# Group averages through small resident matrices, and a last convolution stage in four parts, in a fused channel-attention and selective-scan kernel

## The chip, the cores and the metric

The kernel runs on one core of one Trainium2 chip, in fp32 throughout. The metric is the device time of one execution in microseconds (us), as the median of several runs. TensorE (PE) does products, VectorE (DVE), ScalarE (ACT) and GpSimd (POOL) do elementwise work, and SyncE (SP) issues nearly all DMAs. Each engine takes its own instructions in order and waits on semaphores for the others.

## The reference

The input x is 8 images of 384 channels and 64 x 64 pixels. Two residual layers follow one another, each behind a group normalisation with 32 groups of 12 channels:

```
# layer 0
g = group_norm(x)                      # 32 groups of 12 channels
q, k, v = (dwconv3x3(conv1x1(g, w), dw) for each of the three)
attn = softmax(l2norm(q) @ l2norm(k).T * temperature)   # 8 heads, 48 x 48 channels each
x = x + conv1x1(attn @ v, wproj)
# layer 1
g = group_norm(x)
y = selective_scan of g in four directions (row, column, and both reversed), 16 states
x = x + gelu(layer_norm_over_channels(y merged))
```

A group's mean is the mean of its 12 channels' means; its variance is the mean over the 12 channels of (channel variance + squared distance of the channel mean from the group mean).

## The kernel before, in words

The eight images (batches) run one after another. The 384 channels are three blocks of 128 partitions (NJ = 3, indices j and m), and an image is three resident tiles x[j] of 128 x 4096 elements.

**Attention** (`channel_attention`) runs for one batch at a time. `norm_factors` turns per-channel statistics into mean and rstd per channel. It loads a 384 x 384 averaging matrix avg (576 KB, L113), aggregates the statistics on DVE (L116), multiplies avg with the channel means on PE (L124: seven products, those of each block and its neighbours, since groups of 12 straddle blocks), forms the distance of each channel's mean (L128 to L131), multiplies avg with that (L136, seven products again), and takes the root on ACT (L141). An fp32 product appears in the trace as two PE instructions. Then the 1x1 weights are scaled by rstd (L195), and the three convolutions k, q, v follow. A piece of a convolution (`conv`) is a run of products (L223), their evacuation by ACT (L228), the centre tap on ACT (L232) and eight taps on DVE (L244), each a pass over the whole piece. k and q use pieces of 64 or 32 rows. v is done in three parts, of rows 0 to 32, 32 to 48 and 48 to 64, each for the three blocks; an edge row is carried from one part to the next, and every part but the last computes one row more than it writes.

Woven into the v stage are two other things. `project_out` multiplies the attention matrix, already folded with wproj into mT, with 512 columns of v (L353: three products, one for each block of v), adds the result to x on DVE (L358), takes its statistics (L359) and stores it (L360). A part's projections are put on a list and taken off it, six at a time, during the next part; what is left on the list after the last part is done at the end. And for batches 1 to 7 `finish_part` (L872 to L894) completes 1/16 of the previous batch's layer 1: two loads, scaling on ACT, transposes on PE (L888), gelu on ACT (L889), an add on DVE (L893) and a store. Two of these are emitted behind each of the first eight pieces of v, in two shared buffers. `token_norm` (L862 to L869) takes the statistics for them earlier, from loads fy of the previous batch's result.

**The scan** (`selective_scan`) then calls `norm_factors` with the new statistics, scales x in place (L421, L426), and works through 32 steps of 8 periods each. Its order is written out by hand and pinned. In its last periods it loads the next batch's x and takes its statistics. Its last act is to store y (L658).

Outside the scan a planner decides the order on each engine: it takes instructions by program order and by when it reckons that their inputs are ready, and the order it finds is then fixed. Buffers are shared by tag; an instruction that writes a shared buffer waits for the last reader of the earlier content, and the tiles of a stage wait for the memory of the stage before. The tag "wt" has two buffers, used in turn by avg (in the attention's call of `norm_factors`), wk, wq, wv and wproj. The convolutions and the projections share three PSUM banks (tag "pc").

Of the kernel before, what the change touches and what calls it, by code (L numbers as in the profile page):

```python
# [9 lines left out]
F32 = mybir.dt.float32  # L10
# [5 lines left out]
P = 128  # L16
C = 384
NJ = C // P
H = W = 64
L = H * W  # L20
CH = 512
# [1 line left out]
NT = L // P  # L23
HEADS = 8
HC = C // HEADS
GROUP = C // 32
K = 4
R = 12
N = 16
# [11 lines left out]
GN_EPS = 1e-5  # L41
# [13 lines left out]
BW = max(hi - lo for lo, hi in BANDS)  # L55
# [7 lines left out]
def _constants():  # L63

    c = np.arange(C)
    same = (c[:, None] // GROUP == c[None, :] // GROUP).astype(np.float32)
    avg = (same / np.float32(GROUP)).reshape(NJ, P, C).transpose(1, 0, 2)
    mask = np.zeros((P, NJ, BW), np.float32)
    for i, (lo, hi) in enumerate(BANDS):
        rows = (i * P + np.arange(P)) // HC  # L70
        cols = (lo + np.arange(BW)) // HC
        mask[:, i] = np.where(rows[:, None] == cols[None, :], 0.0, MASKED)
    return np.ascontiguousarray(avg), mask


@with_exitstack
def tile_channel_attention_then_selective_scan(ctx: ExitStack, tc: tile.TileContext, a: dict):
# [10 lines left out]
    pair = const.tile([P, HP], F32, name="pair")  # L88
    twos = ident.rearrange("p (l v) -> p l v", v=2)
    nc.vector.tensor_add(pair, twos[:, :, 0], twos[:, :, 1])  # L90
    ones = const.tile([P, P], F32, name="ones")
    nc.gpsimd.memset(ones, 1.0)
    eps = const.tile([P, 1], F32, name="eps")
# [13 lines left out]
    for j in range(NJ):  # L107
        nc.vector.tensor_scalar_mul(skip[:, j, :], ident, d_sum[:, j : j + 1])

    def norm_factors(pool, psum, stats, tag, bank, home={}):  # L110

        avg = pool.tile([P, NJ, C], F32, name=f"avg{tag}", **home)
        nc.sync.dma_start(avg, a["avg"])  # L113
        mv = pool.tile([P, NJ, 2], F32, name=f"mv{tag}")
        for j in range(NJ):
            nc.vector.bn_aggr(mv[:, j, :], stats[:, j].rearrange("p c s -> p (c s)"))  # L116
        mean = pool.tile([P, NJ], F32, name=f"mean{tag}")
        rstd = pool.tile([P, NJ], F32, name=f"rstd{tag}")
        var = pool.tile([P, NJ], F32, name=f"var{tag}")
        pm = psum.tile([P, CH], F32, tag=bank, name=f"pm{tag}")  # L120
        for j in range(NJ):
            src = [i for i in range(NJ) if abs(i - j) <= 1]
            for i in src:
                nc.tensor.matmul(  # L124
                    pm[:, j : j + 1], lhsT=avg[:, i, j * P : (j + 1) * P], rhs=mv[:, i, 0:1],
                    start=i == src[0], stop=i == src[-1],
                )
        nc.vector.tensor_copy(mean, pm[:, 0:NJ])  # L128
        nc.vector.tensor_sub(var, mv[:, :, 0], mean)
        nc.vector.tensor_mul(var, var, var)  # L130
        nc.vector.tensor_add(var, var, mv[:, :, 1])  # L131
        pv = psum.tile([P, CH], F32, tag=bank, name=f"pv{tag}")
        for j in range(NJ):
            src = [i for i in range(NJ) if abs(i - j) <= 1]
            for i in src:
                nc.tensor.matmul(  # L136
                    pv[:, j : j + 1], lhsT=avg[:, i, j * P : (j + 1) * P], rhs=var[:, i : i + 1],
                    start=i == src[0], stop=i == src[-1],
                )
        nc.vector.tensor_scalar_add(rstd, pv[:, 0:NJ], GN_EPS)  # L140
        nc.scalar.activation(rstd, rstd, AF.Sqrt)  # L141
        nc.vector.reciprocal(rstd, rstd)
        return mean, rstd
# [19 lines left out]
    def channel_attention(b, x, stats, before):  # L163
# [5 lines left out]
        with ExitStack() as st:  # L169
# [4 lines left out]
            ps_a = st.enter_context(tc.tile_pool(name=f"pa{b}", bufs=2, space=PSUM))  # L174
            ps_m = st.enter_context(tc.tile_pool(name=f"pm{b}", bufs=1, space=PSUM))

            mean, rstd = norm_factors(wp, ps_m, stats, f"0_{b}", "misc", dict(tag="wt", bufs=2))

            dws = {}
            for n in ("k", "q", "v"):  # L180
# [94 lines left out]
            for m in range(NJ):  # L275
                acc = work.tile([P, L], F32, tag="acc", name=f"ak{b}{m}")
                parts = (0, H // 2, H) if m == 0 else (0, H)
                for y0, y1 in zip(parts, parts[1:]):
                    conv("k", wk, bk, m, y0, y1, acc[:, y0 * W : y1 * W])
                for t4 in range(NT // 4):  # L280
                    to_tokens(acc, t4, kT[:, 4 * t4 : 4 * t4 + 4, bass.ts(m, P)], f"k{b}{m}")
                r = inverse_norm(acc, f"k{b}{m}")
                diag = work.tile([P, P], F32, tag="diag", name=f"diag{b}{m}")
                nc.vector.tensor_scalar_mul(diag, ident, r)
                pr = ps_a.tile([P, CH], F32, tag="pa", name=f"pr{b}{m}")
                nc.tensor.matmul(pr[:, :P], lhsT=ones, rhs=diag, start=True, stop=True)
                nc.scalar.copy(rks[:, bass.ts(m, P)], pr[:, :P])
# [4 lines left out]
            for m in range(NJ):  # L292
                lo, hi = BANDS[m]
                wd = hi - lo
                acc = work.tile([P, L], F32, tag="acc", name=f"aq{b}{m}")
                parts = (0, H // 2, H) if m == NJ - 1 else (0, H)
                for y0, y1 in zip(parts, parts[1:]):
                    conv("q", wq, bq, m, y0, y1, acc[:, y0 * W : y1 * W])
                pa = ps_a.tile([P, CH], F32, tag="pa", name=f"pa{b}{m}")
                for t4 in range(NT // 4):  # L300
                    qT = work.tile([P, 4, P], F32, tag="qT", name=f"qT{b}{m}_{t4}")
                    to_tokens(acc, t4, qT, f"q{b}{m}")
                    for i in range(4):
                        t = 4 * t4 + i
                        nc.tensor.matmul(
                            pa[:, :wd], lhsT=qT[:, i, :], rhs=kT[:, t, lo:hi],
                            start=t == 0, stop=t == NT - 1,
                        )
                r = inverse_norm(acc, f"q{b}{m}")
                nc.vector.tensor_mul(r, r, small["temp"][:, m : m + 1])  # L310
                lg = work.tile([P, BW], F32, tag="lg", name=f"lg{b}{m}")
                nc.vector.tensor_mul(lg[:, :wd], pa[:, :wd], rks[:, lo:hi])
                nc.vector.scalar_tensor_tensor(
                    lg[:, :wd], lg[:, :wd], r, mask[:, m, :wd], ALU.mult, ALU.add
                )
                mx = work.tile([P, 1], F32, tag="mx", name=f"mx{b}{m}")
                nc.vector.reduce_max(mx, lg[:, :wd], axis=AX.X)
                nc.vector.tensor_scalar_mul(mx, mx, -1.0)
                sm = work.tile([P, 1], F32, tag="sm", name=f"sm{b}{m}")
                nc.scalar.activation(lg[:, :wd], lg[:, :wd], AF.Exp, bias=mx, accum_out=sm)  # L320
                nc.vector.reciprocal(sm, sm)
                nc.vector.tensor_scalar_mul(attn[:, m, lo:hi], lg[:, :wd], sm)
# [24 lines left out]
            x1_d = dram.tile([NJ, P, L], F32, tag="x1d", bufs=2, name=f"x1d{b}")  # L347
            stats1 = big.tile([P, NJ, NCH, nc.vector.BN_STATS_DIM], F32, tag="st1", name=f"st1{b}")

            def project_out(m, c):  # L350
                pc = ps_c.tile([P, CH], F32, tag="pc", name=f"pp{b}{m}_{c}")
                for j in range(NJ):
                    nc.tensor.matmul(  # L353
                        pc, lhsT=mT[:, j, bass.ts(m, P)], rhs=v[:, j, bass.ts(c, CH)],
                        start=j == 0, stop=j == NJ - 1,
                    )
                s = x[m][:, bass.ts(c, CH)]
                nc.vector.tensor_add(s, s, pc)  # L358
                nc.vector.bn_stats(stats1[:, m, c, :], s)  # L359
                nc.sync.dma_start(x1_d[m, :, bass.ts(c, CH)], s)  # L360


            parts = (0, H // 2, 3 * H // 4, H)
            todo, left, edges = [], list(range(L // FT)) if emit else [], {}
            for y0, y1 in zip(parts, parts[1:]):
                for m in range(NJ):
                    pre = conv("v", wv, bv, m, y0, y1, v[:, m, y0 * W : y1 * W], edges.get(m))
                    if y1 < H:
                        edges[m] = work.tile([P, W], F32, tag="edge", bufs=4, name=f"edge{b}{m}_{y1}")
                        o = (y1 - 1 - max(0, y0 - 1)) * W  # L370
                        nc.scalar.copy(edges[m], pre[:, o : o + W])
                    if m > 0:
                        for _ in range(min(len(todo), 6)):
                            project_out(*todo.pop(0))
                    for _ in range(min(len(left), 2)):
                        emit(left.pop(0))
                todo += [(m, c) for c in range(y0 * W // CH, y1 * W // CH) for m in range(NJ)]
            for t in todo:
                project_out(*t)
        return x, x1_d, stats1  # L380

    def selective_scan(b, x1, stats1):
# [535 lines left out]
def _layout(i):  # L918
    def blocks(t, lead):
# [2 lines left out]
        return np.ascontiguousarray(t.reshape(NJ, P, *t.shape[1:]).swapaxes(0, 1))  # L922

    i = {k: np.asarray(v) for k, v in i.items()}
    avg, mask = _constants()
    B = i["x"].shape[0]
    return {
        "x": np.ascontiguousarray(i["x"]).reshape(B, NJ, P, L),
# [13 lines left out]
        "ln_w": blocks(i["L1_conv_ln_weight"], 0),  # L942
        "ln_b": blocks(i["L1_conv_ln_bias"], 0),
        "ident": np.eye(P, dtype=np.float32),
        "avg": avg,
        "mask": mask,
    }

# [16 lines left out]
```

## Time and profile before

| | |
|---|---|
| median of 3 runs (lowest to highest) | 20747.19 us (20741.09 to 20748.04) |
| the profiled execution's own time | 20748.06 us |
| its span, first to last instruction | 20746.3 us |
| PE busy | 19205.9 us (93%) |
| DVE busy | 19321.9 us (93%) |
| ACT busy | 17951.9 us (87%) |
| POOL busy | 15441.2 us (74%) |
| mean granted clock of PE | 0.969 |

The shares are averages over two kinds of stage: POOL has 3.4 us of work in 466 us of a batch's attention and is busy nearly all through the scan. So a stage's limit has to be read from that stage. In the lines below, a time is in us from the start of the span; a line of the timeline has its start, its duration, engine, line, operation, output and input tiles, the count of merged instructions, and in brackets how long the engine stood idle ahead of it and what ended that. Digits in a tile's name are the batch (pc7v: the v convolution of batch 7). PEld is PE's weight load. The ends of products are modelled, so sums of durations on PE overlap a little. A wait on several things is put down to the one that came last by the profile, which need not be the one that mattered.

### The profile page before, as it was taken

The page shows a single profiled execution, that of the slowest core. Times are in us where ns is not written, and L with a number is a line of the kernel's source. Part 1 is how long each engine was busy: PE and PEld are TensorE (multiplying, and loading weights), DVE is VectorE, ACT ScalarE, POOL GpSimd, SP SyncE. Part 2 cuts the span into 40 slices and gives each one's busy share as a digit, 9 for nine tenths or more (in the row PEclk, how much of TensorE's full clock was granted, in tenths as well). Part 3 has the DMA queues.
Part 4 walks back from the last instruction along what each step waited for, and adds up shares of the span by engine and source line. Part 5 has one row for each costly group of instructions (what it writes and reads, how often), then busy time and mean ns, then how long its engine had stood idle before and what let it go on. Part 6 is the DMA issues. An engine that isn't in the chain of part 4 may idle for free. (4 is left out here: it accounts for less than half of the span.)

```text
span 20746.3 us, 319602 instructions
## 1 busy us (share of the span) xinstructions
PE 19205.9 (93%) x118256; PEld 10578.6 (51%) x118256; DVE 19321.9 (93%) x17310; ACT 17951.9 (87%) x32267; POOL 15441.2 (74%) x6918
## 2 busy tenths in 40 slices
PE   7999979999899998999989999899998999989998
PEld 4555545555455554555545555455554555545554
DVE  8999989999899998999989999899998999989998
ACT  3999949999599995999859998599985999859998
POOL 0899808998189981899819997199972999729997
PEclk8999989999899998999989999899998999989999
DMA  1232322323223232232322323223232232322223
GB/s 40 76 92 92 101 77 77 92 93 101 75 80 92 92 104 70 80 92 93 105 68 80 92 92 105 70 80 92 92 103 71 81 93 92 98 74 82 92 92 117
DMA packets 953164, 1807.96 MB, mean 87 GB/s; under 512 B 125905, under 2 KB 646353, under 8 KB 945457
## 3 DMA queue, kind: packets, MB, share of 16 engines
q1 hardware_dynamic: 950736, 1787.40, 27.2%
q8 instruction: 933, 15.29, 0.3%
q14 instruction: 631, 5.16, 0.1%
q10 hardware_dynamic: 864, 0.12, 0.0%
HBM read 1468.39 MB, written 318.77 MB: 86 GB/s over the span
## 5 line engine op out<-in xcount | busy, mean ns | idle before, releaser
L557 POOL TENSOR_TENSOR db<-w,B 128x1536 f32<-128x1536 f32 x4088 | 14143.8, 3467 | 566.6 <-DVE h L569 238.8
L569 DVE TENSOR_TENSOR_SCAN h<-da,ca,db 128x512 f32<-128x512 f32 x10752 | 13058.6, 1267 | 500.2 <-issue 204.3
L603 ACT ACTIVATE hc<-pt,ct 128x384 f32<-128x384 f32 x15128 | 8437.0, 579 | 346.5 <-PE pt L591 287.5
L548 ACT ACTIVATE da<-dt,neg_a 128x512 f32<-128x512 f32 x12288 | 8504.5, 695 | 166.3 <-DVE h L569 134.2
L591 PE MATMUL pt<-ident,h 128*128 128x128 f32 x49152 | 7976.9, 287 | 457.5 <-ACT hc L603 305.0
L591 PEld LDWEIGHTS pt<-ident,h 128*128 128x128 f32 x49152 | 5145.5, 140 | 5115.7 <-ACT hc L603 2549.8
L626 PE MATMUL py<-hc,pair 128*64 128x384 f32 x24576 | 5327.1, 512 | 9.1 <-DVE ys L677 9.1
L406 POOL MEMSET wdt<- 128x1536 f32 x8 | 11.0, 1378 | 3621.5 <-DMA x1d<-x 3621.5
L569 DVE TENSOR_TENSOR_SCAN h<-da,db 128x512 f32<-128x512 f32 x1536 | 1811.5, 1231 | 145.2 <-ACT da L548 75.6
L632 PE MATMUL py<-hc,pair 128*64 128x128 f32 x24576 | 1871.6, 281 | 0.0
L626 PEld LDWEIGHTS py<-hc,pair 128*64 128x64 f32 x24576 | 1216.6, 135 | 1014.6 <-issue 945.3
L455 PE MATMUL px<-x,wx 128*44 128x128 f32 x6144 | 1501.7, 338 | 35.4 <-ACT x L421 29.1
L632 PEld LDWEIGHTS py<-hc,pair 128*64 128x64 f32 x24576 | 1377.2, 136 | 267.2 <-issue 240.2
L532 POOL TENSOR_TENSOR w<-x,dt 128x512 f32<-128x512 f32 x744 | 1057.9, 1422 | 0.0
L455 PEld LDWEIGHTS px<-x,wx 128*44 128x44 f32 x6144 | 635.0, 121 | 817.1 <-issue 771.9
L583 POOL COPY ca<-h 128x6 f32<-128x6 f32 x1792 | 344.2, 192 | 828.4 <-DVE h L569 817.2
L514 PE MATMUL pd<-xd,wdt 128*128 128x512 f32 x1536 | 781.5, 618 | 87.6 <-ACT hc L603 81.8
L605 DVE TENSOR_SCALAR hc<-pt,ct 128x384 f32<-128x384 f32 x1256 | 741.1, 607 | 106.2 <-PE pt L591 61.1
L353 PE MATMUL pp<-v,mT 128*128 128x512 f32 x1152 | 553.9, 634 | 123.5 <-DVE v L244 57.3
L524 ACT ACTIVATE dt<-pd,dt_bias 128x512 f32<-128x512 f32 x768 | 475.4, 686 | 21.3 <-PE pd L514 17.7
L514 PEld LDWEIGHTS pd<-xd,wdt 128*128 128x128 f32 x1536 | 275.3, 192 | 401.3 <-ACT hc L603 199.7
L353 PEld LDWEIGHTS pp<-v,mT 128*128 128x128 f32 x1152 | 228.3, 205 | 403.0 <-issue 312.1
(315 smaller groups left out, 11713.7 us busy)
## 6 DMA issues: line engine op xcount, KB each, us to landing
B<-bcd SPq DMA_DIRECT2D x2048, 512.0 KB
yd<-ys SPq DMA_DIRECT2D x128, 576.0 KB
ys<-yd SPq DMA_DIRECT2D x256, 288.0 KB
yd<-ys SPq DMA_DIRECT2D x256, 288.0 KB
x<-in_x SPq DMA_DIRECT2D x48, 1024.0 KB
x1d<-x SPq DMA_DIRECT2D x192, 256.0 KB
fy<-yd SPq DMA_DIRECT2D x128, 384.0 KB
fin<-yd SPq DMA_DIRECT2D x112, 384.0 KB
```

The source lines that it names most:

```text
L353: nc.tensor.matmul(pc, lhsT=mT[:, j, bass.ts(m, P)], rhs=v[:, j, bass.ts(c, CH)], start=j == 0, stop=j == NJ - 1,)
L455: pin(nc.tensor.matmul(split(pxs[s][:XR, :])[:, part, :], lhsT=wx[:, j, k, :], rhs=view(x1[j], k, c)[:, part, :], start=i == 0, stop=i == ...
L514: pin(nc.tensor.matmul(pds[j], lhsT=wdt[:, k, bass.ts(j, P)], rhs=xds[s], start=True, stop=True))
L532: pin(eng.tensor_mul(split(ws[s][:, j, :]), view(x1[j], k, c), split(dts[s][:, j, :])))
L548: pin(nc.scalar.activation(t, dts[s][:, j, :], AF.Exp, scale=neg_a[:, j, k, n : n + 1]))
L557: pin(eng.tensor_mul(t, ws[g // NP], bts[g][:, v : v + 1, :].broadcast_to([P, NJ, CH])))
L569: pin(nc.vector.tensor_tensor_scan(h, da, db, 0.0 if start else carries[s - 1][:, j, n : n + 1], ALU.mult, ALU.add,))
L591: pin(nc.tensor.transpose(t[:, bass.ts(j, P)], h2s[g][:, j, bass.ts(q, HP), :].rearrange("p l v -> p (l v)"), ident))
L603: pin(eng.activation(out, src, AF.Copy, scale=scale))
L605: pin(eng.tensor_scalar_mul(out, src, scale))
L626: pin(nc.tensor.matmul(py[f * HP : (f + 1) * HP, lb, :C], lhsT=pair, rhs=hc[:, f, :], **flags))
L632: pin(nc.tensor.matmul(py[f * HP : (f + 1) * HP, j, C:], lhsT=pair, rhs=hc[:, f, bass.ts(j, P)], **flags,))
```

## The change

It has four pieces.

- **Group averages.** avg is gone. Two small matrices are loaded once at the start, on SP ahead of x: to_groups (384 channels to 32 groups, with the factor 1/12) and from_groups (32 groups back to 384 channels). An average is now three accumulating products into 32 partitions, a copy on DVE to SBUF, and three products back. Both are done for the mean and for the variance, so each call of `norm_factors` has twelve products where it had fourteen, two more copies, and no load.
- **v in four parts:** rows 0 to 32, 32 to 48, 48 to 56 and 56 to 64. The list then holds three projections at the end, where it held six.
- **The last projections** are one call of `project_out` for all three places: it issues the products of blocks 0 and 1 of v for each of the three, then those of block 2, then the adds.
- **Room:** the work tiles diag and lg have one buffer where they had two.

```diff
-    def norm_factors(pool, psum, stats, tag, bank, home={}):
-        avg = pool.tile([P, NJ, C], F32, name=f"avg{tag}", **home)
-        nc.sync.dma_start(avg, a["avg"])
+    to_groups = const.tile([P, NJ, GROUPS], F32, name="to_groups")
+    nc.sync.dma_start(to_groups, a["to_groups"])
+    from_groups = const.tile([GROUPS, C], F32, name="from_groups")
+    nc.sync.dma_start(from_groups, a["from_groups"])
...
+    def norm_factors(pool, psum, stats, tag, bank):
...
-        pm = psum.tile([P, CH], F32, tag=bank, name=f"pm{tag}")
-        for j in range(NJ):
-            src = [i for i in range(NJ) if abs(i - j) <= 1]
-            for i in src:
+        def average(src, name):
+            pg = psum.tile([P, CH], F32, tag=bank, name=f"{name}g{tag}")
+            for j in range(NJ):
                 nc.tensor.matmul(
-                    pm[:, j : j + 1], lhsT=avg[:, i, j * P : (j + 1) * P], rhs=mv[:, i, 0:1],
-                    start=i == src[0], stop=i == src[-1],
+                    pg[:GROUPS, :1], lhsT=to_groups[:, j, :], rhs=src[j],
+                    start=j == 0, stop=j == NJ - 1,
                 )
-        nc.vector.tensor_copy(mean, pm[:, 0:NJ])
+            g = pool.tile([GROUPS, 1], F32, name=f"{name}s{tag}")
+            nc.vector.tensor_copy(g, pg[:GROUPS, :1])
+            pm = psum.tile([P, CH], F32, tag=bank, name=f"{name}{tag}")
+            for j in range(NJ):
+                nc.tensor.matmul(
+                    pm[:, j : j + 1], lhsT=from_groups[:, bass.ts(j, P)], rhs=g,
+                    start=True, stop=True,
+                )
+            return pm[:, :NJ]
+        nc.vector.tensor_copy(mean, average([mv[:, j, 0:1] for j in range(NJ)], "pm"))
...
-            mean, rstd = norm_factors(wp, ps_m, stats, f"0_{b}", "misc", dict(tag="wt", bufs=2))
+            mean, rstd = norm_factors(wp, ps_m, stats, f"0_{b}", "misc")
...
-                diag = work.tile([P, P], F32, tag="diag", name=f"diag{b}{m}")
+                diag = work.tile([P, P], F32, tag="diag", bufs=1, name=f"diag{b}{m}")
...
-                lg = work.tile([P, BW], F32, tag="lg", name=f"lg{b}{m}")
+                lg = work.tile([P, BW], F32, tag="lg", bufs=1, name=f"lg{b}{m}")
...
-            def project_out(m, c):
-                pc = ps_c.tile([P, CH], F32, tag="pc", name=f"pp{b}{m}_{c}")
-                for j in range(NJ):
-                    nc.tensor.matmul(
...
+            def project_out(*places):
+                pcs = {}
+                for m, c in places:
+                    pcs[m, c] = ps_c.tile([P, CH], F32, tag="pc", name=f"pp{b}{m}_{c}")
+                for js in ((0, 1), (2,)):
+                    for m, c in places:
+                        for j in js:
+                            nc.tensor.matmul(
+                                pcs[m, c], lhsT=mT[:, j, bass.ts(m, P)], rhs=v[:, j, bass.ts(c, CH)],
+                                start=j == 0, stop=j == NJ - 1,
+                            )
+                for m, c in places:
+                    s = x[m][:, bass.ts(c, CH)]
+                    nc.vector.tensor_add(s, s, pcs[m, c])
+                    nc.vector.bn_stats(stats1[:, m, c, :], s)
+                    nc.sync.dma_start(x1_d[m, :, bass.ts(c, CH)], s)
...
-            parts = (0, H // 2, 3 * H // 4, H)
+            parts = (0, H // 2, 3 * H // 4, 7 * H // 8, H)
...
-                            project_out(*todo.pop(0))
+                            project_out(todo.pop(0))
...
-            for t in todo:
-                project_out(*t)
+            assert len(todo) == NJ
+            project_out(*todo)
```

More of the change, by code (lines that the diff above doesn't have):

```diff
@@ L25 @@
 HC = C // HEADS
-GROUP = C // 32
+GROUPS = 32
+GROUP = C // GROUPS
 K = 4
@@ L65, in _constants @@
     c = np.arange(C)
-    same = (c[:, None] // GROUP == c[None, :] // GROUP).astype(np.float32)
-    avg = (same / np.float32(GROUP)).reshape(NJ, P, C).transpose(1, 0, 2)
+    member = (c[:, None] // GROUP == np.arange(GROUPS)[None, :]).astype(np.float32)
+    to_groups = (member / np.float32(GROUP)).reshape(NJ, P, GROUPS).transpose(1, 0, 2)
     mask = np.zeros((P, NJ, BW), np.float32)
@@ L72, in _constants @@
         mask[:, i] = np.where(rows[:, None] == cols[None, :], 0.0, MASKED)
-    return np.ascontiguousarray(avg), mask
+    return np.ascontiguousarray(to_groups), np.ascontiguousarray(member.T), mask
 @with_exitstack
@@ L131, in norm_factors @@
         nc.vector.tensor_add(var, var, mv[:, :, 1])
-        pv = psum.tile([P, CH], F32, tag=bank, name=f"pv{tag}")
-        for j in range(NJ):
[L134 to L140, printed above, removed]
+        nc.vector.tensor_scalar_add(
+            rstd, average([var[:, j : j + 1] for j in range(NJ)], "pv"), GN_EPS
+        )
         nc.scalar.activation(rstd, rstd, AF.Sqrt)
@@ L348, in channel_attention @@
             stats1 = big.tile([P, NJ, NCH, nc.vector.BN_STATS_DIM], F32, tag="st1", name=f"st1{b}")
-            def project_out(m, c):
-                pc = ps_c.tile([P, CH], F32, tag="pc", name=f"pp{b}{m}_{c}")
[L352 to L360, printed above, removed]
-            parts = (0, H // 2, 3 * H // 4, H)
+            def project_out(*places):
[8 more added lines that the diff above has]
+                                start=j == 0, stop=j == NJ - 1,
+                            )
+                for m, c in places:
[4 more added lines that the diff above has]
+            parts = (0, H // 2, 3 * H // 4, 7 * H // 8, H)
             todo, left, edges = [], list(range(L // FT)) if emit else [], {}
@@ L924, in _layout @@
     i = {k: np.asarray(v) for k, v in i.items()}
-    avg, mask = _constants()
+    to_groups, from_groups, mask = _constants()
     B = i["x"].shape[0]
@@ L944, in _layout @@
         "ident": np.eye(P, dtype=np.float32),
-        "avg": avg,
+        "to_groups": to_groups,
+        "from_groups": from_groups,
         "mask": mask,
```

## The prediction

> **What bounds the kernel now.** I read the page first: each batch is about 465 us of attention and 2115 us of scan. The scan keeps its own rhythm and the change leaves it alone, so what counts is the attention stretch and the two seams where one waits for the other. The busy time by stretch, taken over the attention of batch 7 (columns: stretch, its us, then busy us of PE, PEld, DVE, ACT, POOL, then clock and DMA), says who sets it:
>
> ```profile
> 18062.00:18528.00 466.00, 366.63 (x1246) 204.96 (x1246) 401.23 (x336) 204.93 (x375) 3.37 (x4) 0.86 0.25 79
> ```
>
> DVE is busy 401 of 466 us, PE 367, ACT 205. So work moved onto ACT is hidden; work added on DVE, or latency where DVE stands idle, is not. Then the timelines of the two seams, engine by engine. The opening seam (start us, duration, instruction, count, idle before and its releaser), on SP, DVE and PE:
>
> ```profile
> 18062.79 2.85 SPq L658 DMA_DIRECT2D yd<-ys  x4
> 18068.54 0.34 SPq L113 DMA_DIRECT2D avg<-in_avg  x1
> ...
> 18070.82 0.43 SPq L188 DMA_DIRECT2D wk<-in_wk  x1
> 18080.17 0.38 SPq L188 DMA_DIRECT2D wq<-in_wq  x1
> ```
>
> ```profile
> 18068.60 0.83 DVE L116 BATCH_NORM_AGGREGATE mv<-st 128x2 f32<-128x48 f32 x3 [0.48 <-DVE st L160]
> ```
>
> ```profile
> 18072.97 3.12 PE L124 MATMUL pm<-mv,avg 128*128 128x1 f32 x14 [12.12 <-DMA dwv<-in_dwv]
> 18077.02 3.12 PE L136 MATMUL pv<-var,avg 128*128 128x1 f32 x14 [0.93 <-DVE var L131]
> ```
>
> The statistics are ready at 18069.43, the averaging products start at 18072.97: 3.54 us in which nothing runs. Its releaser is named dwv, but a product reads only mv and avg, so it is the 576 KB of avg, issued at 18068.54 when the last y store lets the memory go. The same gap in batches 1 to 7 is 3.21, 3.58, 3.59, 3.27, 3.21, 4.64, 3.54: 25.0 us. In batch 0 avg is there before the last statistics.
>
> The closing seam, PE then DVE:
>
> ```profile
> 18489.74 5.42 PE L223 MATMUL pc7v<-x,wv 128*128 128x512 f32 x12
> 18495.00 5.31 PE L353 MATMUL pp<-v,mT 128*128 128x512 f32 x12
> 18507.48 13.18 PE L353 MATMUL pp<-v,mT 128*128 128x512 f32 x24 [7.17 <-DVE v L244]
> ...
> 18522.58 1.03 PE L124 MATMUL pm<-mv,avg 128*128 128x1 f32 x6 [1.13 <-DVE mv L116]
> 18524.46 3.15 PE L136 MATMUL pv<-var,avg 128*128 128x1 f32 x14 [0.84 <-DVE var L131]
> ```
>
> ```profile
> 18497.10 10.23 DVE L244 SCALAR_TENSOR_TENSOR v<-pre7v,dwv,v 128x1008 f32<-128x1008 f32 x8 [1.59 <-ACT v L232]
> 18509.56 0.69 DVE L358 TENSOR_TENSOR x<-x,pp 128x512 f32<-128x512 f32 x1 [2.23 <-PE pp L353]
> ...
> 18522.15 0.37 DVE L116 BATCH_NORM_AGGREGATE mv<-st 128x2 f32<-128x48 f32 x1
> ```
>
> An fp32 product is two instructions. The 12 at 18495.00 are six products: three projections already have two of their three products done while DVE still runs the last taps. The 24 after the taps are the three missing products and three whole projections. From last tap (18507.34) to last aggregate (18522.52) is 15.2 us.
>
> **What the Trainium skill says.** "TensorE: Matmul & The Clock Gate", section "What's actually happening": after about 3.4 us idle PE falls to half clock and needs about 3.4 us of work to recover. The trace agrees: after 7.17 us idle the 24 took 13.18, where 0.43 each (5.31/12) would be 10.3. The same page, "LDWEIGHTS": a weight load goes by columns, not rows. The trace agrees only weakly (44 columns, L455, mean 121 ns against 140 for 128, L591), so I give the 32-column loads no discount. "VectorE: DVE Perf Modes", section on the errata of SBUF-source operations: each instruction pays a fixed extra. Agrees: taps of 2016 elements 2.316 us, of 1008 1.264, so 1.04 ns an element and 0.21 us fixed.
>
> **The change part by part,** against the profiled execution's 20748.06 us (span 20746.3; it stands 0.9 above the median 20747.19).
>
> (a) Opening seam, batches 1 to 7. The 25.0 us wait goes; mv still waits for the y store, so statistics end where they did. The chain after them: before, 14 instructions, 3.15 with latency. After, two to-group products run while aggregates 2 and 3 finish; then 2 instructions x 0.223 (3.12/14) = 0.45, copy 0.2, latency 0.17, six from-group instructions 1.34: 2.2. Gain 0.95. For the variance: before 3.30; after 6 x 0.223 + 0.2 + 0.14 + 1.34 + 0.2 = 3.2. Gain 0.1. So 25.0 + 7 x 1.05 = 32, less latency 0.4: -32. Cover: wk must be in by 18077.6, when the new rstd is due. The same table of stretches, cut finer, shows the DMA engines nearly still (0.11) from 18077 on:
>
> ```profile
> 18077.00:18082.00 5.00, 3.12 (x14) 3.05 (x14) 0.16 (x1) 1.49 (x2) 0.00 (x0) 0.50 0.11 23
> ```
>
> so wk, behind avg and mask, had landed by then, and lands earlier without avg. If a 32-row product were half as costly, another 1.3 a batch; if new forms cost double, 4 back: bounds -41 and -4... I take -32, and hold -26 to -38 likely. wq no longer waits for avg's buffer (18080.17 becomes about 18071), and the 16 fy loads queued behind it on SP start 9 us earlier. I book nothing: the token statistics fill DVE gaps that are there anyway.
>
> (b) Batch 0: two small loads ahead of x on SP, 2 x 0.39, and the extra hop 0.5 minus 0.1: +1 (0 to +2).
>
> (c) Closing seam norm, PE not yet cold: before 6 x 0.17 after the last aggregate (1.12 with latency), after 2 x 0.17 + 0.2 + 0.17 + 6 x 0.17 = 1.75; variance as in (a). +0.6 x 8 = +5 (+2 to +8). On DVE the two copies wait for PE; behind them stand only the next steps of the same chain.
>
> (d) Four parts. The last 16 rows, one part of 8 taps x 3 blocks at 1.28 (30.7), become two of 8 rows: 24 taps of about 504 elements at 0.74 + 0.02, and 24 with some of 441: 18.2 + 17.6, less 14 that overlap with adds by 0.1: 34.4. So DVE gets 3.7 more. PE gets three one-row halos (0.78 each), ACT three more edge copies and evacuations (busy 205 of 466: hidden). Batch 7, from the end of part two on DVE (18461.7): the first small piece is ready at 18462.5 (before 18465.25). Then taps 34.4, nine projections' add and statistics at 1.21 = 10.9, four finish adds at 0.87 = 3.5, and an idle before block 2 of the third part: PE needs 6 x 2.58 for six projections, 1.3 for transposes, then 3.4 for the piece, ACT 1.2; DVE is done 3.1 before. Last tap 18514.4, later than before. After it six instructions instead of 24: 5.8 us to the last aggregate if PE is warm, 7.25 if cold; I take 6.5: 18520.9 against 18522.52. With one finish add falling into the idle, -2 to -2.5; I take -2. Without the idle -5; if the piece waits behind the last finish part's transposes (18489.39 today) +3. Batch 0 has no finish parts: before 404.3 to 466.5; after 405.9 + 34.4 + 10.9 + 2 + 6.5 = 459.7: -6.5. Together -6.5 - 14 = -20 (-42 to +20). The two-ahead order itself is booked at 0, as the planner already does it for three tiles; forcing it matters only if it would stop.
>
> (e) One buffer for diag and lg: diag's reader (L286 at 18149.96) is done 73 us before the next write (18222.84), lg's last reader (18304.39) 12 us before L312 at 18316.51. 0; were the cover gone, DVE would wait 1 to 2 us for PE or ACT. The stores of x1d are issued in the same number and nothing on the path waits for them; wx and wdt behind them keep 7 us or more to their first use, since they hang on the last projection as before.
>
> Sum: -32 + 1 + 5 - 20 = -46: 20702 in the profiled execution, 20701 as a median.
>
> **Rivals.** (1) The tail gains in full: DVE never idles in parts three and four, PE stays warm: (d) is -7 - 7 x 5 = -42, in all -68: 20679. For it: 5.5 us of DVE idle today in that stretch. Against it: the six projections need 15.5 us of PE where DVE has about 13 of work. (2) The tail gives nothing: the added DVE time and the idle eat the shorter ending; (d) between -5 and +20: 20716 to 20741, centre 20725. For it: the last tap moves later. (3) Slower: the planner sets the small pieces of v behind the finish transposes on PE. These arrive at the pace of two buffers (load, ACT, PE, store: about 14 us a pair), and PE takes products in order, so DVE would stand for one such arrival per batch. It decides from +3.3 a batch in (d) on (26 of gains elsewhere over 8), and passes 0.2% at (26 + 41.5) / 8 = 8.4. At 10 us: 20748 - 26 + 80 = 20802. Against it: today the piece of block 2 runs as soon as products are out. (4) That the copies of avg were not late at all: excluded by the seven gaps.
>
> **How the numbers follow.** Forecast 0.42 (20690 to 20715, most of it beyond 0.2%), rival 1 0.24, rival 2 0.26, rival 3 0.08. 0.2%, about what a measurement of this kernel tells from no change, is 41.5 us: the line lies at 20705.7. Of the forecast 0.36 lies below it; so faster 0.60, same 0.32, slower 0.08. The range, 20665 to 20736, takes rival 1 with a warm opening seam and rival 2 but its worst end; both sides outside hold 0.2.
>
> **What would show it.** Right: L124's successor starts within 0.1 us of the aggregate in batches 1 to 7; rstd 4.6 us after the same statistics sooner; six product instructions after the last tap. Wrong: a first product still released by a DMA, a DVE idle over 5 us before the last two pieces, or another order in the k and q convolutions.

## The result, and the profile after

| | before | after |
|---|---|---|
| median (lowest to highest), us | 20746.92 (20739.25 to 20750.37), 13 runs | 20697.19 (20687.47 to 20706.35), 13 runs |
| ratio, 95% interval | | 0.9977 (0.9969 to 0.9985) |
| profiled execution, its span | 20748.06, 20746.3 | 20697.19, 20695.1 |

The change takes 50 us, 0.23%. The forecast was 20701. The sum came out, but most of its terms did not: one missed by 32 us in one direction, and several smaller ones, two of them not booked at all, happened to make up for it. Cutting both traces at the same seven events of every batch and adding up the eight batches gives the account (us, after minus before):

| stretch | sum | by batch | forecast |
|---|---|---|---|
| start to the last aggregate, batch 0 | -2.3 | | with the next row, batch 0: +1 |
| last aggregate to rstd, opening seam | -40.3 | batch 0 -0.5; batches 1 to 7 -5.3 to -6.7 | batches 1 to 7: -32 |
| rstd to the first tap of v | -10.4 | -0.3 to -2.4 | 0 |
| first tap of v to its last tap | +85.3 | batch 0 +1.4; batches 1 to 7 +11.8 to +12.2 | with the next row: -20 |
| last tap to the last aggregate | -73.2 | -8.5 to -9.4 | |
| last aggregate to rstd, closing seam | -1.0 | -0.9 to +1.2 | +5 |
| the scan, and the end | -9.1 | -2.6 to +1.1 | 0 |
| all | -51.1 | | -46 |

The last tap comes later and the ending is shorter, as the forecast had it. But the two together come to -7.5 us in batch 0 and to +2.4 to +3.7 in each of the others (+12.0 in all), where -20 was booked.

The stretches of batch 7's attention in the kernel after (us, then busy us of PE, PEld, DVE, ACT, POOL, clock, DMA) show DVE as the busiest engine still, 404 of 462 us, where it was 401 of 466:

```profile
18018.00:18480.00 462.00, 365.92 (x1256) 203.68 (x1256) 404.31 (x365) 208.73 (x388) 3.37 (x4) 0.87 0.24 77
```

The opening seam of batch 7 after, on SP, DVE and PE (start us, duration, instruction, count, idle before and releaser):

```profile
18018.75 2.85 SPq L673 DMA_DIRECT2D yd<-ys  x4
...
18026.11 0.44 SPq L197 DMA_DIRECT2D wk<-in_wk  x1
18026.59 0.49 SPq L197 DMA_DIRECT2D wq<-in_wq  x1
```

```profile
18024.38 0.83 DVE L120 BATCH_NORM_AGGREGATE mv<-st 128x2 f32<-128x48 f32 x3 [0.31 <-DMA yd<-ys]
```

```profile
18024.96 0.58 PE L129 MATMUL pmg<-mv,to_groups 128*32 128x1 f32 x6 [8.16 <-DVE mv L120]
18025.77 1.44 PE L137 MATMUL pm<-pms,from_groups 32*128 32x1 f32 x6 [0.24 <-DVE pms L134]
18028.14 0.45 PE L129 MATMUL pvg<-var,to_groups 128*32 128x1 f32 x6 [0.93 <-DVE var L146]
18028.83 1.44 PE L137 MATMUL pv<-pvs,from_groups 32*128 32x1 f32 x6 [0.24 <-DVE pvs L134]
```

The first product is now released by DVE, not by a DMA, and starts before the last of the three aggregates ends (18025.21); before, it started 3.54 us after that end. The six instructions to groups take 0.45 to 0.58 us together, the six from groups 1.44.

The closing seam of batch 7 after, PE from the third part on, then DVE:

```profile
18436.68 0.44 PE L903 MATMUL pz<-ident,fin 128*128 128x128 f32 x2 [1.87 <-ACT fin L896]
18436.95 0.78 PE L232 MATMUL pc7v<-x,wv 128*128 128x64 f32 x6
...
18463.64 2.84 PE L367 MATMUL pp<-v,mT 128*128 128x512 f32 x6 [1.58 <-DVE v L253]
18468.09 2.81 PE L367 MATMUL pp<-v,mT 128*128 128x512 f32 x6 [1.61 <-DVE v L253]
18473.40 0.64 PE L129 MATMUL pmg<-mv,to_groups 128*32 128x1 f32 x6 [2.49 <-issue]
```

```profile
18433.72 0.96 DVE L908 TENSOR_TENSOR fin<-fin 128x768 f32<-128x768 f32 x1 [0.70 <-ACT fin L904]
18440.82 0.96 DVE L908 TENSOR_TENSOR fin<-fin 128x768 f32<-128x768 f32 x1 [6.13 <-ACT fin L904]
18441.69 10.22 DVE L253 SCALAR_TENSOR_TENSOR v<-pre7v,dwv,v 128x504 f32<-128x504 f32 x15
...
18461.00 6.95 DVE L253 SCALAR_TENSOR_TENSOR v<-pre7v,dwv,v 128x504 f32<-128x504 f32 x10 [0.80 <-ACT v L241]
18469.23 0.69 DVE L373 TENSOR_TENSOR x<-x,pp 128x512 f32<-128x512 f32 x1 [1.28 <-PE pp L367]
...
18472.94 0.82 DVE L120 BATCH_NORM_AGGREGATE mv<-st 128x2 f32<-128x48 f32 x3
```

Six instructions follow the last tap, in 2.81 us, and the ending takes 5.81 us instead of 15.06 (batch 1). What pays for it is the 6.13 us ahead of the last finish add (5.9 to 6.7 in batches 1 to 7). The chain behind it, on SP and then ACT:

```profile
18424.29 0.38 SPq L909 DMA_DIRECT2D out<-fin  x1
...
18427.10 0.50 SPq L894 DMA_DIRECT2D fin<-x1d  x1
18428.51 1.63 SPq L375 DMA_DIRECT2D x1d<-x  x2
18430.26 0.41 SPq L893 DMA_DIRECT2D fin<-yd  x1
18430.71 0.47 SPq L894 DMA_DIRECT2D fin<-x1d  x1
```

```profile
18435.92 1.31 ACT L896 ACTIVATE fin<-fin,fsh,fsc 128x384 f32<-128x384 f32 x2 [2.22 <-DMA fin<-x1d]
```

The last finish part's load is issued at 18430.26, 6.0 us after the store of the part two before it, with which it shares a buffer. ACT scales it at 18435.92. The transposes that need it (18436.68) stand on PE ahead of the 64-column products of the halo row (18436.95), which the third block's piece needs before DVE can run its taps. All of the third block's taps of that part wait for a load of the previous batch.

The shared buffer is not what held the load last. In the 2.6 us between the load at 18427.10 and this one, SP waits for DVE alone, by the view of its waits (`--waits --engine SP --window 18427.7:18430.8`: instruction, what it waited for, us in total, times, longest):

```profile
SPq L375 <- DVE x L373: 1.8, 2, 1.0
```

The two stores of x1d (L375) stand ahead of the load in SP's order and wait for adds on DVE. In each of batches 1 to 7 the last load is issued right behind such a store, 6.0 us after the store of its buffer. What an earlier place for it on SP would give was not tried; it could be issued up to 2.6 us earlier, an estimate from the lines above.

### The profile page after: what moved, and what is told of

The parts are those of the page before. It is cut to its first block, busy times and chain, and to the rows that moved or that the text cites. A ratio compares the mean times of both kernels' runs of the same rounds, so it can differ in the third digit from the quotient of the medians.

```text
span 20695.1 us, 320057 instructions
## 1 busy us (share of the span) xinstructions
PE 19201.8 (93%) x118336; PEld 10567.8 (51%) x118336; DVE 19346.5 (93%) x17534; ACT 17969.7 (87%) x32363; POOL 15446.0 (75%) x6918
## 4 chain that ended last, share of the span: by engine, by line
ACT 45%; PE 25%; DVE 20%; issue 6%; POOL 3%; DMA 1%; SPq 0%; DVEq 0%; ACTq 0%; POOLq 0%
ACT hc L618 24%; ACT da L563 20%; PE pt L606 9%; DVE h L584 7%; PE py L641 6%; DVE aq L253 3%; DVE v L253 3%; POOL db L572 3%; DVE ak L253 3%; PE py L647 2%; PE pp L367 2%; DVE ys L692 2%; PE px L470 1%; DVE hc L620 1%; PE py L633 1%
```

## The experiments

**The two parts of the change, each alone.** First the group averages without the four parts. `project_out` is that of the kernel before, not shown here; the single buffers of diag and lg stay:

```diff
-            parts = (0, H // 2, 3 * H // 4, 7 * H // 8, H)
+            parts = (0, H // 2, 3 * H // 4, H)
...
-            assert len(todo) == NJ
-            project_out(*todo)
+            for t in todo:
+                project_out(*t)
```

> Theory 1 (the gain is the group averages): the kernel before with the new group averages and nothing else. Opening seam about -40 over the eight batches, first batch's start -2, closing seam's norm about 0 to +5 and no loss in the third part: 20685 to 20705 us, at or a few us below the changed kernel's 20697. Rival (the tail's four parts and ready products carry the gain): within 10 us of the kernel before, 20737 to 20757.

Measured 20695.27 us, ratio 0.9978 (0.9969 to 0.9987), inside the first theory's range: 46.4 below the 20741.64 of the kernel before beside it. The opening seam has -40.3 in all, the same as in the whole change. From first tap to last aggregate it is +2.5 in all.

Then the four parts and the grouped projections without the averages (`project_out` is that of the change):

```diff
-            parts = (0, H // 2, 3 * H // 4, H)
+            parts = (0, H // 2, 3 * H // 4, 7 * H // 8, H)
...
-            for t in todo:
-                project_out(*t)
+            assert len(todo) == NJ
+            project_out(*todo)
```

> Theory 1: the kernel before with four parts and grouped last projections, the group averages as before. From the changed kernel's trace: about -7.5 us in the first batch, +2.5 in each of the other seven, so +5 to +15: 20752 to 20762 us. Rival (the step as I had booked it): -20, so 20727 us. Second rival (tail in full): -42, so 20705 us.

Measured 20746.17 us beside 20741.64 of the kernel before, ratio 1.0002 (0.9994 to 1.0010): +4.5 us, just under the first theory's +5 to +15. -20 lies outside the interval, whose lower end is -12. In its trace, from first tap to last aggregate, batch 0 gains 7.5 and each of the other seven loses 0.5 to 4.2: +11.7 in all. (The profiled execution was this kernel's slowest, 14 us over its median.) So the whole measured gain is the averages'; the four parts, which were to bring 20, bring none. Behind the shorter ending the closing norm with the old averages also takes 8.0 us more; the averages alone make it 1.5 longer, both together 1.0 shorter. So the two parts are not quite independent there.

**What the opening seam lost: a wait or dearer products?** The two small matrices are fetched inside each norm again:

```diff
-    to_groups = const.tile([P, NJ, GROUPS], F32, name="to_groups")
-    nc.sync.dma_start(to_groups, a["to_groups"])
-    from_groups = const.tile([GROUPS, C], F32, name="from_groups")
-    nc.sync.dma_start(from_groups, a["from_groups"])
...
     def norm_factors(pool, psum, stats, tag, bank):
+        to_groups = pool.tile([P, NJ, GROUPS], F32, name=f"tog{tag}")
+        nc.sync.dma_start(to_groups, a["to_groups"])
+        from_groups = pool.tile([GROUPS, C], F32, name=f"fromg{tag}")
+        nc.sync.dma_start(from_groups, a["from_groups"])
```

> The changed kernel, with the two small group matrices fetched within each norm instead of once. Theory 1 (what the opening seam lost was a load that landed late): the two loads stand behind the same stores on SP and bring back a wait of at least one small transfer's 2 to 3 us in batches 1 to 7, up to the old seam's 5 to 6: +15 to +40 against the changed kernel, 20712 to 20737 us, with the first products after the last aggregate starting later than 1 us behind it. Rival (the seam is shorter because the products are fewer and narrower): no change within 5 us, 20692 to 20702.

Measured 20707.62 us, ratio 0.9984 (0.9977 to 0.9990), 10.4 over the changed kernel; the opening seams of batches 1 to 7 are 10.2 longer, 1.2 to 1.8 each. That is outside the rival's 5, but also below the 15 to 40 that the wait theory gave: a wait came back, smaller than forecast. In batch 7 the load is issued at 18028.52, the aggregates end at 18029.34, and PE starts here:

```profile
18030.73 0.45 PE L129 MATMUL pmg<-mv,tog 128*32 128x1 f32 x6 [9.77 <-POOL attn L300]
```

That is 2.21 us after the issue, of which the aggregates cover 0.82: 1.39 us after they end, where avg of 576 KB made it 3.54 and resident matrices make it less than nothing. (The releaser named here cannot be it: attn is done long before.) So of the 39.8 us in batches 1 to 7, 25.0 were the wait for avg, and a load of a twelfth of its size would have brought back 10. The rest, 2 us a batch, is the products. For the mean, from the point where they may start to its copy on DVE, it was 3.15 (batch 1, before) and is 2.04 (batch 7, after). For the variance, from the step on DVE ahead of the products to the one behind them, it was 3.30 and is 2.31.

**The written order of the last projections.**

```diff
-            assert len(todo) == NJ
-            project_out(*todo)
+            for t in todo:
+                project_out(t)
```

> The changed kernel with the last three projections written one after another, as in the kernel before, in place of first two products of each and then the three third ones. Theory 1 (the written order does the work: with one at a time the first group's third product holds the queue before the other groups' first two): last v tap to last aggregate grows from 5.8 us by 2 to 5 in each of eight batches, +16 to +40, 20713 to 20737 us. Rival (the shorter last part alone gives it; the scheduler has the ready products ahead anyway): within 5 us of the changed kernel's 20697.

Measured 20702.12 us, ratio 0.9981 (0.9975 to 0.9988). Last tap to last aggregate is 5.81 us in all eight batches, as in the changed kernel: the rival's outcome. On PE, batch 7:

```profile
18486.21 2.74 PE L367 MATMUL pp<-v,mT 128*128 128x512 f32 x6
18490.53 2.84 PE L367 MATMUL pp<-v,mT 128*128 128x512 f32 x6 [1.59 <-DVE v L253]
18494.98 2.81 PE L367 MATMUL pp<-v,mT 128*128 128x512 f32 x6 [1.61 <-DVE v L253]
```

First the three products of block 0, then of block 1, then of block 2: the planner has the ready ones ahead without being told. The explicit order is worth nothing here; the shorter ending is that of a last part of 8 rows, with three projections and not six.

**Why the four parts do not pay in batches 1 to 7.** The finish parts are left out, once with three parts and once with four (both with the new averages):

```diff
-            todo, left, edges = [], list(range(L // FT)) if emit else [], {}
+            todo, left, edges = [], [], {}
```

> New group averages, three parts and one-at-a-time projections, with the finish parts left out: the outputs of batches 0 to 6 are not computed or written. It is only the base for the four-part kernel without them. From its first v tap to its last aggregate, batches 1 to 7 should then look like batch 0 (within 2 us of it).

> The changed kernel with the finish parts left out (outputs of batches 0 to 6 not computed or written). First v tap to last aggregate, against the three-part kernel without them: theory 1 (finish parts meet the shorter parts and cost what the tail gains) gives batch 0's -7.5 us in every batch, about -60 in all; rival (the extra taps and their fixed cost on VectorE eat the gain by themselves) gives about +2.5 in batches 1 to 7, as with the finish parts.

From first tap to last aggregate, three parts take 167.0 to 167.2 us in every batch and four take 159.6 to 159.9: -7.1 to -7.4 in each, -58 in all, in the seven as in batch 0. Their whole times, 20634.94 and 20622.76 from one execution each, differ by less: the closing norm of the second is 1.3 us longer in each batch, and its scan takes 36 us more in all, which was not followed up. The stretch of batch 3 for both (columns as above):

```profile
7989.39:8156.43 167.04, 121.88 (x287) 54.63 (x285) 143.00 (x125) 27.90 (x47) 1.66 (x2) 0.86 0.10 37
```

```profile
7985.35:8145.16 159.81, 121.65 (x305) 54.99 (x303) 145.22 (x149) 30.27 (x59) 2.31 (x3) 0.88 0.10 39
```

And the same stretch with the finish parts, three parts (the kernel with the averages alone) and then the changed kernel:

```profile
8007.18:8178.91 171.73, 138.63 (x377) 63.63 (x375) 156.24 (x141) 71.52 (x124) 1.66 (x2) 0.88 0.41 137
```

```profile
8005.06:8179.28 174.22, 141.33 (x395) 66.13 (x393) 158.54 (x165) 73.93 (x136) 2.31 (x3) 0.88 0.41 135
```

DVE's busy and idle time say what happens. The extra taps cost 2.2 to 2.3 us in both pairs, and the finish parts 13.2 to 13.3 of busy time. With three parts the finish parts lengthen the stretch by 4.7 only, because DVE's idle time falls from 24.0 to 15.5: they fill waits for v. With four parts they lengthen it by 14.4, because idle time stays (14.6 and 15.7). The four parts had taken those waits away, and the finish parts bring one of their own. That settles that the taps alone are not the loss, and that the gain vanishes only where finish parts meet the four parts.

**Is it that they come late?** Three finish parts behind each piece in place of two, so that all sixteen are done in the first two parts:

```diff
-                    for _ in range(min(len(left), 2)):
+                    for _ in range(min(len(left), 3)):
```

> The changed kernel, with up to three finish parts of the batch before after each quarter of v in place of two, so that none stands behind the products of the last two parts. Theory 1 (the tail's loss is the last finish part's transposes that hold TensorE's queue while their load is late, 6.13 us of VectorE idle in batch 7): the idle time goes, -3 to -6 in each of seven batches, -20 to -40 against the changed kernel: 20657 to 20677 us. Rival (the loss is the fixed cost of more and smaller taps on VectorE): no change within 5 us, 20692 to 20702. A third outcome: the wait moves to an earlier piece, where the loads are as late, and nothing is gained.

Measured 20697.08 us, ratio 0.9979 (0.9971 to 0.9987): nothing, the third outcome. Batch 3's 6.48 us of idle DVE is gone, but the first taps of part two wait 4.74 instead of 3.24 and those of part three's last block 2.73. Over the eight batches the taps end 13.8 us sooner after they began, the ending is 7.3 longer and the closing norm 4.2. The reason for the longer ending, in batch 7:

```profile
18470.53 2.84 PE L367 MATMUL pp<-v,mT 128*128 128x512 f32 x6 [1.89 <-DVE v L253]
18475.78 4.40 PE L367 MATMUL pp<-v,mT 128*128 128x512 f32 x6 [2.40 <-DVE v L253]
```

PE idles 1.89 and then 2.40 us until taps end on DVE, and the last six take 4.40 us in place of 2.81, at a lower clock. Cut at the step of the clock (columns as in the stretches above):

```profile
18475.78:18478.90 3.12, 3.12 (x4) 1.48 (x5) 1.01 (x2) 0.00 (x0) 0.00 (x0) 0.50 0.00 0
18479.00:18480.18 1.18, 1.17 (x3) 0.19 (x1) 0.96 (x2) 0.00 (x0) 0.00 (x0) 1.00 0.57 222
```

Why PE idles longer there than in the changed kernel (1.58 and 1.61) was not followed up.

**Is a short part the trouble?** Parts of 32, 24 and 8 rows keep the short ending with one set of taps less, with three finish parts a piece and with two:

```diff
-            parts = (0, H // 2, 3 * H // 4, 7 * H // 8, H)
+            parts = (0, H // 2, 7 * H // 8, H)
```

> The changed kernel with three parts of 32, 24 and 8 rows, up to three finish parts per piece (nine in the first part, seven in the long second). The third set of 27 taps' fixed cost goes (about 0.2 us each on VectorE, some 3 to 5 us per batch), the tail stays 5.8 us if its products run at the same speed. Theory 1 (finish parts in a long part cost nothing): -7 to -10 in each batch against the changed kernel's first v tap to last aggregate, 20620 to 20660 us. Rival (the ring of two finish buffers is too slow for three per piece, as where three per piece were tried with four parts, and the wait opens elsewhere): -0 to -3 per batch, 20675 to 20697.

> Three parts of 32, 24 and 8 rows with three finish parts per piece, once more beside the changed kernel on one chip: 20670 us, 20 to 35 below it.

> The changed kernel with parts of 32, 24 and 8 rows and two finish parts per piece, so that four of the sixteen fall into the part of 8 rows. Theory 1 (finish parts in a short part are what cost): most of the gain of the same parts with three per piece (27 us) is lost, -10 to +10 against the changed kernel, 20687 to 20707 us, with an idle stretch of 3 to 7 us on VectorE in the last part of batches 1 to 7. Rival (the gain of that kernel is the nine taps per row block that it saves, wherever the finish parts stand): 20665 to 20677 us, as with three per piece.

> The changed kernel itself, on the chip of the two kernels beside it, as their base: 20697 us, within 5.

Three a piece: 20669.65 us, ratio 0.9966 (0.9952 to 0.9979), between the two theories; once more 20669.28, 0.9962 (0.9949 to 0.9976). Two a piece: 20662.22, 0.9961 (0.9948 to 0.9973), beside 20695.56, 0.9976 (0.9967 to 0.9985), for the changed kernel on the same chip. So my theory missed, and the rival's time is met and a little passed: of the 4.7 to 6.4 us that batches 1 to 7 gain from first tap to last aggregate, 4.4 are taps saved (DVE busy 154.10 instead of 158.54 in batch 3). With four finish parts in a part of only 8 rows, DVE waits there 0.70 and 2.63 us, not 6.48. DVE in batch 3, in the changed kernel and then in this one:

```profile
8146.39 0.96 DVE L908 TENSOR_TENSOR fin<-fin 128x768 f32<-128x768 f32 x1 [6.48 <-ACT fin L904]
```

```profile
8139.73 0.96 DVE L908 TENSOR_TENSOR fin<-fin 128x768 f32<-128x768 f32 x1 [0.70 <-ACT fin L904]
8143.32 1.53 DVE L253 SCALAR_TENSOR_TENSOR v<-pre3v,dwv,v 128x504 f32<-128x504 f32 x2 [2.63 <-ACT v L241]
...
8146.03 0.95 DVE L908 TENSOR_TENSOR fin<-fin 128x768 f32<-128x768 f32 x1
```

The last part has no halo row. On PE the piece's products start at 8138.94 and the late transposes at 8142.02, so they are over before these come, and the last finish add stands among taps. The last load is as late here, 5.0 to 6.8 us behind its buffer's store. So a short part with finish parts in it need not wait for them; the question is what stands behind the late load. (The ending is 2 us longer, 8.2 in batch 1: nine projections of the 24 rows are on PE's queue with three more.)

**The order itself.** Four parts as in the change, but none of the last four finish parts behind the third part's first block:

```diff
-                    for _ in range(min(len(left), 2)):
+                    for _ in range(0 if (y0, m) == (3 * H // 4, 0) else min(len(left), 2)):
```

> The changed kernel, with no finish parts behind the first block of the third part of v: its four stand behind the second and third block. In the written order of TensorE, the third block's products of that part then stand behind transposes of the first two of these finish parts, whose buffers and loads are free early, and no longer behind those of the last one. Theory 1 (the 6.1 to 6.5 us that VectorE stands idle there is that last part's late load, in front of the halo products): the idle time falls to 1 to 3 us, -3 to -5 in each of batches 1 to 7, 20660 to 20675 us. Rival (the pair of buffers is the pace wherever the parts stand): the same 6 us open one part later, in front of the last part's projections, 20690 to 20705 us.

Measured 20670.09 us, ratio 0.9964 (0.9950 to 0.9977), in the first theory's range. First tap to last tap: batch 0 +0.3, batches 1 to 7 -6.0 to -6.5. DVE, batch 3:

```profile
8127.26 0.96 DVE L908 TENSOR_TENSOR fin<-fin 128x768 f32<-128x768 f32 x1 [0.59 <-ACT fin L904]
8129.04 0.96 DVE L908 TENSOR_TENSOR fin<-fin 128x768 f32<-128x768 f32 x1 [0.83 <-ACT fin L904]
8130.64 8.49 DVE L253 SCALAR_TENSOR_TENSOR v<-pre3v,dwv,v 128x504 f32<-128x504 f32 x12 [0.64 <-ACT v L241]
8139.05 0.95 DVE L908 TENSOR_TENSOR fin<-fin 128x768 f32<-128x768 f32 x1
...
8142.61 0.95 DVE L908 TENSOR_TENSOR fin<-fin 128x768 f32<-128x768 f32 x1
```

The finish adds and taps are as many (DVE is busy 158.85 us from first tap to last aggregate, against 158.54), the 6.48 is gone, and the last two adds fall without a wait. The edit also moves the load on SP: no store of x1d stands between the last two stores of finish parts and their loads, and the last load is issued 2.8 us behind its buffer's store, not 6.0:

```profile
8128.24 2.17 SPq L909 DMA_DIRECT2D out<-fin  x2
8130.85 0.37 SPq L893 DMA_DIRECT2D fin<-yd  x1
8131.27 0.50 SPq L894 DMA_DIRECT2D fin<-x1d  x1
8132.80 0.36 SPq L893 DMA_DIRECT2D fin<-yd  x1
```

So this run shows that the loss hangs on the place of the finish parts. It does not tell the order on PE from the order on SP. The run with 32, 24 and 8 rows speaks for PE: there the load stayed late and the wait was 2.63. Of the 6.2 a batch, 1.2 to 2.5 are given back at the end, where PE idles 3.18 us and the last six take 4.48:

```profile
8152.17 2.84 PE L367 MATMUL pp<-v,mT 128*128 128x512 f32 x6 [0.65 <-DVE v L253]
8158.19 4.48 PE L367 MATMUL pp<-v,mT 128*128 128x512 f32 x6 [3.18 <-DVE v L253]
```

This kernel and the one with 32, 24 and 8 rows beat both kernels of the case by one line each. Both lines together were not tried.

## Why the prediction was right or wrong

- **(a) Opening seam: right in kind, 8 us too small.** The 25.0 us wait went, and the first product starts before the last aggregate ends, as its signs of being right had it. The failed term is "for the variance: 3.2, gain 0.1", and the 0.223 per instruction to groups under it. I had refused the 32-column loads a discount. The median weight load of avg took 291 ns for the mean and 333 for the variance, of to_groups 117 and 157 ns: the six took 0.45 us, not 1.34. The Trainium skill, "TensorE: Matmul & The Clock Gate", section "LDWEIGHTS (loading the stationary operand)", was right here (a weight load goes by columns), and the weak reading I set against it was of other loads, in other stages. Fewer rows saved nothing: six products of 32 rows took 1.44, where 1.34 is booked for six of 128.
- **(b) Batch 0: sign wrong, 3.8 us.** +1 booked, -2.3 and -0.5 measured. The x loads do start 0.95 us later. But Ds is issued at 1.66 us before and 1.67 after on ACT's queue, and its sum on DVE, which waits for it, starts at 9.87 before and at 4.45 after. The first statistics, which stand behind that sum, began at 7.82 instead of 10.84. That the x transfers had held it up fits the order of issue and was not tested alone.
- **(c) Closing norm: +5 booked, -1.0 measured.** Alone with three parts +1.5. The hop cost 0.25 us in batch 7 (last aggregate to the copy of the mean 1.13, now 1.38), and the cheaper products of the variance gave 1.00 back (3.24, now 2.24).
- **(d) Four parts: -20 booked, +12.0 measured, and this is the wrong step.** Its -6.5 for batch 0 (-7.5) and its ending (6.5; 5.8) held. The taps cost 2.3 more, not 3.7. What failed is "an idle before block 2 of the third part: DVE is done 3.1 before", for batches 1 to 7. Measured in batch 7 are 1.08, 0.70 and 6.13; an idle of over 5 us was among my own signs of being wrong. I had let PE run the piece as soon as it had room; the halo products stood behind a late load's transposes, which I had named only as the bad end ("+3") and, grown to 8 a batch, as rival 3. The truth was +2.4 to +3.7 a batch. Rival 3's mechanism was at work below the point where it decides, and the size, +12.0, is that of rival 2, whose range for (d) was -5 to +20.
- **(e) Single buffers: no wait on them shows in the seams. x1d's stores: wrong.** I wrote that "nothing on the path waits for them", but on SP the last finish part's load stands behind two of them (18428.51 in batch 7), and that load is on the path.
- **What was not booked.** rstd to the first tap of v is 10.4 us shorter in all. The nine other runs with the new averages and the finish parts, one of them the changed kernel again at -6.0, have -10.7 to +2.9 there, seven of them -5 to -11; the one with the old averages has +1.2. wq, no longer behind avg's buffer, is issued 1.4 us after the last aggregate of batch 7 instead of 10.7; whether that is the reason was not tried. The 9.1 us of the scan lie within the 19 us by which executions of this one kernel differ.
- **Two sums were slightly off.** 5.31/12 is 0.44, not 0.43, which makes the warm time of the 24 instructions 10.6. The figures for batch 0 in (d) give -6.8, not -6.5. Neither moves the forecast.

So the total was right because 8 us more at (a), 4 at (b), 6 at (c) and some 20 unbooked stood against the 32 missed at (d). The mechanism of (a), the wait for avg, was right; that of (d) was not, and that the sum met the measurement all the same was luck.

## What to carry to other kernels

When a stage is cut finer, look for work of another stream that is interleaved at a fixed number per piece: the same number falls on half the time, and one late load of that stream then holds an in-order engine for both. A wait filled by such side work is not free to be removed: taking it away gains only what the side work did not already use. Look also at the queue that issues that stream's loads: here stores that wait for another engine stood ahead of the load that mattered. And shrinking a constant's load is not the same as keeping the constant resident: a transfer a twelfth as large still cost 1.2 to 1.8 us of the seam each time.

## What the runs showed of the hardware that was not expected

- Products are taken in order: the Trainium skill says so in "TensorE: Matmul & The Clock Gate", section "The mechanism" (matmuls are "strict FIFO, no reordering"), and the halo products behind the transposes at 18436.68 agree.
- Idle stretches of 2.40 us (with 1.89 just before) and of 3.18 were enough to lower the granted clock: six products took 4.40 and 4.48 us, against 2.81 after 1.61. The clock stood at 0.50 for the first 3.2 and 3.4 us of them and at 1.00 after that, 0.64 and 0.63 over the six. The section "What's actually happening" of the same page states half clock after at least one idle window of about 3.4 us. The half agrees; the gaps were shorter than that window. It gives about 3.4 us of sustained work to recover; in the kernel before, the 24 instructions behind 7.17 us of idle ran at 0.50 for 5.3 us.
- A load of 48 KB issued 0.8 us ahead of its need kept PE waiting 1.4 us; one of 576 KB issued 0.9 us ahead, 3.5.
